# Hybrid attention and state-space kernel: three of the skips' seven products added up in PSUM, seven products for one more batch of queries, and new prices for GpSimd in the planner

## The chip, the cores and the metric

The kernel runs on one core of one Trainium2 chip. The metric is the device time of one execution in microseconds (us); "before" is the median of three runs. A profile is one further execution with the hardware profiler on. The engines are PE (TensorE, its weight loads shown as PEld), DVE (VectorE), ACT (ScalarE), POOL (GpSimd) and SP (SyncE, which issues nearly all the transfers here).

## The reference

Four layers act on `x`, a tensor of 4 sequences of 1024 tokens with 256 features, all in float32; each layer normalizes its input and adds its output to `x`.

```python
x = x + attn_a(layernorm(x), Wq, bq, Wk, bk, Wv, bv)      # causal attention, one head of 256
x = x + ffn(layernorm(x), W_r, W_k, W_v, mu_r, mu_k)      # r * (relu(k)**2 @ W_v), tokens mixed with the one before
x = x + attn_b(layernorm(x), A_log, W_B, W_C, D_skip, log_dt, W_in, b_in, W_out, b_out, ln_g, ln_b)
x = x + ffn(layernorm(x), W_r, W_k, W_v, mu_r, mu_k)      # the same weights again

# attn_b, a state-space layer (xn: the normalized input)
x_proj, z = split(xn @ W_in.T + b_in); z = silu(z)
x_mean = causal_convolution(x_proj @ W_B.T * dt.mean(), decay)   # 16 states
y = x_mean @ W_C.T + D_skip * x_proj
out = (y * z) @ W_out.T + b_out + residual
```

The change touches the queries of the attention and, in the state-space layer, `D_skip * x_proj` (called the skip) and its sum with `x_mean @ W_C.T` (called the states' share).

## The kernel before, in words

**Halves and names.** A sequence (batch `b`, 0 to 3) is worked in two halves of 512 tokens; half `j` runs from 0 to 7, `j = 2*b + h`. A tile of "columns" holds 512 tokens on the free axis and 256 features as two blocks (`c` or `e`, 0 and 1) of 128 partitions. A product of one 128x128 block of weights with 512 columns is one matmul in the code and two PE instructions in the trace.

**Eight or seven products.** A 256x256 weight applied to both halves of a batch is a product of 2x2 blocks: eight block products. `project_columns` (L774 in the trace) does it plainly, four for each half. `seven_products` (L830) does it in seven, by Winograd's scheme. Four of the seven use sums of weight blocks (made once, `weight_sums`), four use sums of data blocks `T1` to `T4` (made for each batch by `stream_sums`, L813, on GpSimd or VectorE). Each product `p1` to `p7` lands in a PSUM bank of its own, and VectorE adds them up (L838 plain, L840 with a bias): `c11 = p1 + p2`, `u2 = p1 + p6`, `u3 = u2 + p7`, `c21 = u3 + p4`, `c22 = u3 + p5`, `c12 = u2 + p5 + p3`. Before the change the queries of batches 2 and 3 (`qs2`, `qs3`), the gates `z` of batches 1 to 3 (`zs1` to `zs3`), the skips of batches 1 to 3 (`ss1` to `ss3`) and the keys of the last layer's batches 0 to 2 (`gks0` to `gks2`) are made so. Queries of batches 0 and 1 are made plainly by `queries` (tiles `pp_a0` to `pp_a3`).

**The states' share.** For batches 1 to 3, `mix_states_apart` multiplies `w_c` with the states in four small matmuls (contraction over 16 rows) into a pair of PSUM banks for each half (`py`, L1889). `grown` adds the skip, already in SBUF, to it on VectorE (L1899); `gated` multiplies by `z` on GpSimd or VectorE (L1903); `state_outputs` multiplies by `w_out` (tiles `pyo`).

**The planner.** No engine's order is written out by hand. The code logs units (a group of matmuls, in the order in which PE runs them) and operations (with what they need, and one or more ways: an engine and a price in us). `Order.finish` then plays the log through with these prices, with several sets of settings, keeps the plan that ends first by its own count, and emits every engine's instructions in that order. A way marked `DVE+port`, and every way of GpSimd, is taken to hold a port that the two engines share: the planner lets only one of them run at a time. PE's order of units is the order of the log; what stands on VectorE, ScalarE, GpSimd and in SP's queue, and when, follows from the prices. In PSUM, four single banks and two pairs are shared out among the units.

**The order of the units.** In the attention, step `i` (0 to 31) covers one tile of 128 queries: scores (`sc`), softmax, transposed weights through DRAM (`exps`, `pblocks`, `prT`), and the weighted sum (`po`). Between them stand values (`pv`), the first feed-forward layer's units (`f0` to `f7`), and the queries: plain ones by `both(queries, j)`, the seven products as a chain whose next product is logged by `go_on` when at least 0.8 us of other units lie between, and whose rest is logged at once ahead of the first scores of that batch. `attend_prepare(n)` puts the normalization of half `n`, its way through DRAM (`rows_a`, `blocks_a`) and its turn to columns (`xa`) into the log:

```python
if i == 4 * n - (12 if n % 2 and n > 2 * SEVEN_FROM else 8):
    attend_prepare(n)
```

After the attention, `more_gates(n)` takes the next `n` products of one long chain (gates and skips of batches 1 to 3), and `advance(keys, n)` the next `n` products of a chain of keys.

Of the kernel before, what the change touches and what calls it, by code (L numbers as in the profile page):

```python
# [15 lines left out]
ALU = mybir.AluOpType  # L16
# [4 lines left out]
NB = 4  # L21
# [14 lines left out]
EXP_ARG_MAX = 88.0  # L36
RPAD = P + L
APART = 0.8
SEVEN_FROM = 2
PLAIN = 1  # L40
BY_SCALAR = 6
AHEAD_FROM = 4
# [307 lines left out]
def hybrid_kernel(  # L350
# [445 lines left out]
    def stream_sums(key, src, needs):  # L796

        t = [lazy(lambda k=k: cols(f"T{k}_{key}")) for k in range(KC)]

        def b(c, h):  # L800
            return src(h)[:, c, :]

        def sums(k):
            return t[(k - 1) // 2]()[:, (k - 1) % 2, :]

        for k, plus, minus in (
            (1, lambda: b(0, 1), lambda: b(0, 0)),
            (3, lambda: b(1, 1), lambda: b(0, 1)),
            (2, lambda: b(1, 1), lambda: sums(1)),
            (4, lambda: b(1, 0), lambda: sums(2)),  # L810
        ):
            def emit(engine, k=k, plus=plus, minus=minus):
                engine.tensor_sub(sums(k), plus(), minus())  # L813

            o.op(
                f"{key}.T{k}", needs + ([f"{key}.T{k - 1}"] if k in (2, 4) else []),
                ("POOL", 1.05, partial(emit, nc.gpsimd)), ("DVE+port", dve(HALF), partial(emit, nc.vector)),
            )
        return sums

# [78 lines left out]
    class Mix:  # L899
# [4 lines left out]
        def prepare(self, j, by_hand=False):  # L904

            b, h = divmod(j, 2)
            key = f"{self.tag}{j}"
            hT = self.hT[j] = lazy(lambda: cols(f"hT_{key}", HALF + 1))
            xk = self.xk[j] = lazy(lambda: cols(f"xk_{key}"))
            xr = self.xr[j] = lazy(lambda: cols(f"xr_{key}"))  # L910
            names = [f"{key}.hT{c}" for c in range(KC)]
            self.rows[j] = normalized(
                key, b, h, self.needs(j), lambda c: hT()[:, c, 1:], names, by_hand=by_hand,
                by_scalar=self.last and j < BY_SCALAR,
            )
            if h == 0:
                first = lambda: nc.gpsimd.memset(hT()[:, :, 0:1], 0.0)
                before = [f"{key}.xn0"]
            else:
                old = self.hT[j - 1]  # L920
                first = lambda: nc.gpsimd.tensor_copy(hT()[:, :, 0:1], old()[:, :, HALF:])
                before = [f"{self.tag}{j - 1}.hT{c}" for c in range(KC)] + [f"{key}.xn0"]
            o.op(f"{key}.h", before, ("POOL", 0.2, first))
            for name, t, mu, mu1 in (("xk", xk, muk, muk1), ("xr", xr, mur, mur1)):
                for c in range(KC):
                    def scale(t=t, mu=mu, c=c):
                        nc.scalar.mul(t()[:, c, :], hT()[:, c, 1:], mu[:, c : c + 1])

                    def add(t=t, mu1=mu1, c=c):
                        nc.vector.scalar_tensor_tensor(  # L930
                            t()[:, c, :], hT()[:, c, :HALF], mu1[:, c : c + 1], t()[:, c, :],
                            ALU.mult, ALU.add,
                        )

                    o.op(
                        f"{key}.{name}m{c}", [names[c], "mu1"],
                        ("ACT", act(HALF), scale),
                        delay=0.0 if name == "xk" else 0.8,
                    )
                    o.op(  # L940
                        f"{key}.{name}{c}", [f"{key}.{name}m{c}", f"{key}.h"],
                        ("DVE+port", dve(HALF) + 0.06, add),
                    )
# [77 lines left out]
        def values(self, j, g):  # L1021
# [28 lines left out]
                f"{key}.rv{g}", [f"{key}.g{g}", f"{key}.pv{g}"], ("DVE", dve(HALF), gate),  # L1050
                frees="bank",
            )
            o.op(f"{key}.x{g}", [f"{key}.rv{g}"], ("POOL", 1.27, add))
            if last:
                o.op(None, [f"{key}.x{g}"], ("SP", 0.47, store), moves=[move(8 * P * D, 1024, True)])

# [809 lines left out]
    def skips_of_batch(b):  # L1866

        there = columns_of(2 * b) + columns_of(2 * b + 1)
        src = lambda h, xb=(xnT[2 * b], xnT[2 * b + 1]): xb[h]()
        for j in (2 * b, 2 * b + 1):  # L1870
            skips[j] = lazy(lambda j=j: cols(f"skip_{j}"))
        sb = [skips[2 * b], skips[2 * b + 1]]
        sums_of_batch(b + 1)
        yield from seven_products(
            f"ss{b}", f"zs{b}", wx_block, lambda k: x_sums[:, k - 1, :], src, sums_of_batch(b),
            lambda e, h: sb[h]()[:, e, :], lambda e: b_skip[:, e : e + 1],
            ["x_sums", "b_all"], there,
        )

    def mix_states_apart(b):  # L1880

        for h in range(2):
            py[2 * b + h] = lazy(lambda h=h: pair(f"py_{2 * b + h}"))

        def emit():
            for e in range(KC):
                for h in range(2):
                    k = 2 * e + h
                    nc.tensor.matmul(  # L1889
                        py[2 * b + h]()[:, ts(e, HALF)],  # L1890
                        lhsT=w_c[k * GRP : k * GRP + S, ts(e, P)],
                        rhs=xmT[b]()[k * GRP : k * GRP + S, ts(h, HALF)],
                        start=True,
                        stop=True,
                    )

        def grown(j, e):
            t = skips[j]()[:, e, :]
            nc.vector.tensor_add(t, py[j]()[:, ts(e, HALF)], t)  # L1899

        def gated(engine, j, e):
            t = z[j]()[:, e, :]
            engine.tensor_mul(t, t, skips[j]()[:, e, :])  # L1903

        o.unit(f"pm{b}", 1.0, ["w_c", f"xmT{b}"], emit, "pair", many=2)
        for h in range(2):
            j = 2 * b + h
            for e in range(KC):
                o.op(
                    f"g{e}.{j}", [f"pm{b}", f"ss{b}.c{e + 1}{h + 1}"],  # L1910
                    ("DVE", dve(HALF) + 0.03, partial(grown, j, e)),
                    frees="pair" if e else None,
                )
                o.op(
                    f"y{e}.{j}", [f"g{e}.{j}", f"z{e}.{j}"],
                    ("POOL", 1.05, partial(gated, nc.gpsimd, j, e)),
                    ("DVE+port", dve(HALF), partial(gated, nc.vector, j, e)),
                )

# [101 lines left out]
    for i in range(-2, NI):  # L2021
# [18 lines left out]
        if 0 < j < 2 * NB:  # L2040
# [5 lines left out]
                    attend_prepare(n)  # L2046
            if k == (1 if i < AHEAD_FROM else 0) and j < 2 * SEVEN_FROM:
                both(queries, j)
            if k == 3 and j % 2 == 1 and SEVEN_FROM <= j // 2 + 1 < NB:
                chain = queries_of_batch(j // 2 + 1)  # L2050
                behind = len(o.log)
        while valued < min(i + (3 if i < AHEAD_FROM else 4), NI - 1):
            valued += 1
# [73 lines left out]
    for b in range(NB):  # L2127
        states_in(b)
    skip(1)
    more_gates(8)  # L2130
    mix_states(0)
    more_gates(8)
    outputs(0)
    more_gates(5)
    mix_states_apart(1)
    outputs(1)
    more_gates(4)
    outputs(2)
    more_gates(4)
    mix_states_apart(2)  # L2140
    outputs(3)
    more_gates(3)
# [13 lines left out]
    keys = mix2.keys_of_batch(1)  # L2156
    both(mix2.gates, 2)
    outputs(7)
    advance(keys, 7)
    both(mix2.gates, 3)  # L2160
    both(mix2.values, 2)
    keys = mix2.keys_of_batch(2)
    both(mix2.values, 3)
# [65 lines left out]
```

## Time and profile before

| | |
|---|---|
| three runs | 464.29, 464.99, 465.58 us; median 464.99 |
| the profiled execution | 465.0 us, of which the span of its instructions is 463.1 |
| PE | busy 456.0 us, 98% of the span |
| PEld (weight loads) | busy 312.5 us, 67% |
| DVE | busy 390.2 us, 84%, 931 instructions |
| ACT | busy 220.8 us, 48%, 463 instructions |
| POOL | busy 143.1 us, 31%, 149 instructions |
| granted TensorE clock | full speed in every slice |

The span begins with the first instruction and ends with the last. A row of the groups names the line, the engine, the operation, what it writes and reads, how often it stands there, its busy time and the mean of one, and then for how long the engine had been idle before it and what ended that. VectorE starts its next instruction before the record of the last one closes: two plain adds in a row, each recorded with 0.68 us, start 0.60 us apart.

### The profile page before, as it was taken

The numbers are of one execution on the slowest core, as the hardware profiler recorded it, in microseconds if no ns is written. First come the engines' busy times: TensorE is split into PE (matmuls) and PEld (weight loads), VectorE is DVE, ScalarE is ACT, GpSimd is POOL, SyncE is SP. The second block draws the span as 40 slices with busy tenths as digits, with TensorE's granted clock in tenths as the row PEclk, the third lists the DMA queues.
The fourth block names the chain that finished last, engine by engine and source line by source line (L and its number), as shares of the span: only waits on it lengthen the run. The fifth ranks groups of instructions, "written<-read, shape, count | busy, mean of one in ns | idle before, by whom it ended". The sixth has DMA issues, their size and how long they took to land.

```text
span 463.1 us, 6634 instructions
## 1 busy us (share of the span) xinstructions
PE 456.0 (98%) x2052; PEld 312.5 (67%) x2052; DVE 390.2 (84%) x931; ACT 220.8 (48%) x463; POOL 143.1 (31%) x149
## 2 busy tenths in 40 slices
PE   8999999999999999999999999999999999999996
PEld 5766785667786667786777775474565758675875
DVE  3687769899969999889999977459889999999962
ACT  3422414454342433333556567441458777664652
POOL 3000102112013213121271354962052616826340
PEclk9999999999999999999999999999999999999999
DMA  8047876848455763427866989603022024252442
GB/s 242 21 127 203 250 190 168 222 132 258 117 135 139 221 194 93 118 62 237 224 177 182 275 268 271 260 17 88 11 92 91 1 86 144 81 147 99 129 144 84
DMA packets 84915, 69.44 MB, mean 150 GB/s; under 512 B 20160, under 2 KB 82576, under 8 KB 84880
## 3 DMA queue, kind: packets, MB, share of 16 engines
q1 hardware_dynamic: 84064, 68.76, 50.8%
q10 hardware_dynamic: 816, 0.26, 0.2%
q8 instruction: 16, 0.26, 0.2%
q14 instruction: 19, 0.16, 0.1%
HBM read 40.54 MB, written 28.45 MB: 149 GB/s over the span
## 4 chain that ended last, share of the span: by engine, by line
PE 86%; DVE 8%; issue 2%; DMA 1%; POOL 1%; ACT 1%; SPq 0%; DVEq 0%; POOLq 0%
PE po L1597 13%; PE sc L1492 13%; PE pv L1464 5%; PE p_zs L830 4%; PE p_ss L830 4%; PE p_qs L830 2%; PE p_gks L830 2%; PE py L1848 2%; PE pc L1798 2%; PE dust L1282 1%; DMA blocks_a<-rows_a 1%; PE pr_g0.pr L881 1%; PE pb L1735 1%; PE pp_a0.pq L774 1%; PE pr_g0.pv L881 1%
## 5 line engine op out<-in xcount | busy, mean ns | idle before, releaser
L1597 PE MATMUL po<-v,prT 128*128 128x256 f32 x288 | 67.7, 380 | 0.1
L1492 PE MATMUL sc<-xa,q 128*128 128x512 f32 (+3 forms) x192 | 67.0, 486 | 0.0
L1597 PEld LDWEIGHTS po<-v,prT 128*128 128x128 f32 x288 | 54.2, 189 | 11.6 <-issue 2.6
L1513 ACT ACTIVATE pr<-pr,nmx 128x128 f32<-128x128 f32 (+7 forms) x32 | 24.7, 773 | 64.6 <-DVE pr L1508 57.7
L1492 PEld LDWEIGHTS sc<-xa,q 128*128 128x128 f32 x192 | 35.1, 190 | 24.5 <-issue 19.6
L1464 PE MATMUL pv<-wv,xa 128*128 128x257 f32 x128 | 32.9, 380 | 0.0
L642 POOL TENSOR_TENSOR rs_a<-ve_a,minus_half 128x4 f32<-128x4 f32 x7 | 7.1, 1010 | 76.8 <-DVE ve_a L629 76.8
L1044 POOL TENSOR_TENSOR x<-x,r_f 128x512 f32<-128x512 f32 x16 | 20.3, 1271 | 33.0 <-DVE r_f L1038 32.5
L642 POOL TENSOR_TENSOR rs_h<-ve_h,minus_half 128x8 f32<-128x8 f32 x8 | 13.2, 1647 | 52.5 <-DVE ve_h L631 52.5
L1464 PEld LDWEIGHTS pv<-wv,xa 128*128 128x128 f32 x128 | 23.6, 191 | 7.8 <-issue 3.6
L1508 DVE TENSOR_SCALAR_CACHE_REDUCE pr<-sc,v 128x128 f32<-128x128 f32 (+7 forms) x32 | 26.2, 818 | 1.1
L1550 DVE STREAM_TRANSPOSE prT<-pblocks 128x384 f32<-128x384 f32 (+7 forms) x30 | 23.8, 793 | 2.4 <-DMA pblocks<-exps 2.3
L642 POOL TENSOR_TENSOR rs_f<-ve_f,minus_half 128x4 f32<-128x4 f32 x8 | 8.4, 1053 | 47.1 <-DVE ve_f L629 28.8
L1044 POOL TENSOR_TENSOR x<-x,r_g 128x512 f32<-128x512 f32 x14 | 18.9, 1371 | 11.0 <-DVE r_g L1038 11.0
L1641 POOL TENSOR_TENSOR x<-x,bout_r 128x512 f32<-128x512 f32 x16 | 20.0, 1279 | 4.5 <-ACT x L1634 4.5
L1606 DVE SCALAR_TENSOR_TENSOR x<-po,rsm,x 128x256 f32<-128x256 f32 x32 | 15.0, 470 | 4.3 <-PE po L1597 3.8
L1474 DVE TENSOR_TENSOR v<-pv,bv_r 128x257 f32<-128x257 f32 x32 | 13.4, 418 | 5.6 <-PE pv L1464 5.6
L930 DVE SCALAR_TENSOR_TENSOR xr_g<-hT_g,mur,xr_g 128x512 f32<-128x512 f32 x16 | 17.3, 1112 | 0.0
L663 ACT ACTIVATE xn_f<-x,mrs_f,rs_f 128x256 f32<-128x256 f32 x18 | 9.8, 592 | 15.5 <-DVE mrs_f L651 15.5
L1634 ACT ACTIVATE x<-x,mrs_h,rs 128x256 f32<-128x256 f32 x32 | 16.9, 592 | 0.0
L1903 POOL TENSOR_TENSOR z<-z,skip 128x512 f32<-128x512 f32 x9 | 13.1, 1462 | 10.9 <-DVE skip L1899 10.7
L663 ACT ACTIVATE xn_g<-x,mrs_g,rs_g 128x256 f32<-128x256 f32 x23 | 12.4, 589 | 8.3 <-DVE mrs_g L626 6.7
(458 smaller groups left out, 1089.8 us busy)
## 6 DMA issues: line engine op xcount, KB each, us to landing
hk<-r_dram SPq DMA_DIRECT2D x16, 512.0 KB, 9.2
rows_g<-xn_g SPq DMA_DIRECT2D x8, 512.0 KB, 2.9
blocks_g<-rows_g SPq DMA_DIRECT2D x32, 128.0 KB, 2.8
x<-in_L_attn_a_X_dram SPq DMA_DIRECT2D x7, 512.0 KB, 4.9
rows_f<-xn_f SPq DMA_DIRECT2D x7, 512.0 KB, 3.0
blocks_f<-rows_f SPq DMA_DIRECT2D x28, 128.0 KB, 2.7
rows_h<-xn_h SPq DMA_DIRECT2D x7, 512.0 KB, 3.7
blocks_h<-rows_h SPq DMA_DIRECT2D x28, 128.0 KB, 3.2
```

The source lines that it names most:

```text
L642: nc.gpsimd.tensor_tensor(rs()[:, :k].rearrange("p k n -> p (k n)"), ve()[:, :k].rearrange("p k n -> p (k n)"), minus_half[:, : k * NH], A ...
L663: nc.scalar.activation(place(n), split(row(n)), AF.Identity, bias=mrs()[:, k - 1, n : n + 1], scale=rs()[:, k - 1, n : n + 1],)
L830: lambda: nc.tensor.matmul(p(), lhsT=w(), rhs=data(), start=True, stop=True), "bank",
L930: nc.vector.scalar_tensor_tensor(t()[:, c, :], hT()[:, c, :HALF], mu1[:, c : c + 1], t()[:, c, :], ALU.mult, ALU.add,)
L1044: nc.gpsimd.tensor_add(xg, xg, r()[:, ts(g, 2), :])
L1464: nc.tensor.matmul(pv()[:, : D + 1], lhsT=xaj()[:, c, ts(n, P)], rhs=wv[:, c, :], start=(c == 0), stop=(c == KC - 1),)
L1492: nc.tensor.matmul(sc()[:, k * HALF : k * HALF + w], lhsT=qh()[:, c, ts(n, P)], rhs=keys[k]()[:, c, :w], start=(c == 0), stop=(c == KC - 1),)
L1508: nc.vector.tensor_scalar(dst, src, v[2 * b + h]()[:, n, D : D + 1], None, ALU.add, ALU.min, accum_out=nmx(),)
L1513: nc.scalar.activation(p()[:, :nk], p()[:, :nk], AF.Exp, bias=nmx(), scale=-1.0, accum_out=sm())
L1550: nc.vector.transpose(dst()[:, : NH * width].rearrange("p (k m a) -> p k m a", m=NH, a=GRP), blocks().rearrange("p m (k a) -> p k m a", a= ...
L1597: nc.tensor.matmul(po()[:, :D], lhsT=src()[:, ts(n, P)], rhs=v[2 * b + n // NH]()[:, n % NH, :D], start=(n == 0), stop=(n == t),)
L1641: nc.gpsimd.tensor_add(xg, xg, bout_r.unsqueeze(1).to_broadcast([P, 2, D]))
```

## The change

1. `SEVEN_FROM` goes from 2 to 1: the queries of batch 1 are made by seven products too. By the line shown above, the preparation of half 3 then enters the log at step 0 and not at step 4.
2. The chains of queries of batches 2 and 3 begin at steps 12 and 20 (`k == 0`, `j` of 4 and 6), one step later than before; that of batch 1 begins at step 4.
3. The skips' `p2`, `p4` and `p3` no longer get a bank and an add of their own. `mix_states_apart` starts each of three PSUM banks with one of them, and the states' matmul adds onto it. `skips_of_batch` keeps `p1`, `p6`, `p7`, `p5` and the adds `u2`, `u3`, `u5`, `u4`; the bias moves into `grown`.
4. The planner's prices for GpSimd change: sums `T` 1.05 to 1.45, the first column `h` 0.2 to 0.28, `x + r` 1.27 to 1.33, `gated` 1.05 to 1.4.
5. The counts of `more_gates` are fitted to the shorter chain, and the last layer's gates of half 3 are set into the chain of keys of batch 1.

```diff
-SEVEN_FROM = 2
+SEVEN_FROM = 1
...
-                ("POOL", 1.05, partial(emit, nc.gpsimd)), ("DVE+port", dve(HALF), partial(emit, nc.vector)),
+                ("POOL", 1.45, partial(emit, nc.gpsimd)), ("DVE+port", dve(HALF), partial(emit, nc.vector)),
...
-            o.op(f"{key}.h", before, ("POOL", 0.2, first))
+            o.op(f"{key}.h", before, ("POOL", 0.28, first))
...
-            o.op(f"{key}.x{g}", [f"{key}.rv{g}"], ("POOL", 1.27, add))
+            o.op(f"{key}.x{g}", [f"{key}.rv{g}"], ("POOL", 1.33, add))
...
     def skips_of_batch(b):
...
-        yield from seven_products(
-            f"ss{b}", f"zs{b}", wx_block, lambda k: x_sums[:, k - 1, :], src, sums_of_batch(b),
-            lambda e, h: sb[h]()[:, e, :], lambda e: b_skip[:, e : e + 1],
-            ["x_sums", "b_all"], there,
-        )
+        u1, u2, u3, u5 = block(0, 0), block(0, 1), block(1, 0), block(1, 1)
+        p = unit(1, lambda: wx_block(0, 0), lambda: xnT[2 * b]()[:, 0, :], there)
+        o.op(f"{key}.u1", [f"{key}.p1"], *copies(u1, p), frees="bank")
+        yield
+        p = unit(6, lambda: x_sums[:, 1, :], lambda: T(2), [f"zs{b}.T2"])
+        add("u2", 6, p, u1, u2, "u1")
+        yield
+        p = unit(7, lambda: x_sums[:, 2, :], lambda: T(3), [f"zs{b}.T3"])
+        add("u3", 7, p, u2, u3, "u2")
+        yield
+        p = unit(5, lambda: x_sums[:, 0, :], lambda: T(1), [f"zs{b}.T1"])
+        add("u5", 5, p, u3, u5, "u3", last=False)
+        add("u4", 5, p, u2, u2, "u3")
+        yield
...
     def mix_states_apart(b):
...
         def emit():
+            for h, e, w, data in (
+                (0, 0, wx_block(0, 1), xnT[2 * b]()[:, 1, :]),
+                (0, 1, wx_block(1, 1), T(4)),
+                (1, 0, x_sums[:, 3, :], xnT[2 * b + 1]()[:, 1, :]),
+            ):
+                nc.tensor.matmul(
+                    py[2 * b + h]()[:, ts(e, HALF)], lhsT=w, rhs=data, start=True, stop=False
+                )
...
-                        start=True,
+                        start=(k == 3),
...
-            nc.vector.tensor_add(t, py[j]()[:, ts(e, HALF)], t)
+            nc.vector.scalar_tensor_tensor(
+                t, py[j]()[:, ts(e, HALF)], b_skip[:, e : e + 1], t, ALU.add, ALU.add
+            )
...
-                    ("POOL", 1.05, partial(gated, nc.gpsimd, j, e)),
+                    ("POOL", 1.4, partial(gated, nc.gpsimd, j, e)),
...
-            if k == 3 and j % 2 == 1 and SEVEN_FROM <= j // 2 + 1 < NB:
-                chain = queries_of_batch(j // 2 + 1)
+            if k == 0 and j in (2, 4, 6):
+                chain = queries_of_batch(j // 2)
...
-    more_gates(8)
+    more_gates(6)
     mix_states(0)
-    more_gates(8)
+    more_gates(5)
     outputs(0)
-    more_gates(5)
+    more_gates(3)
     mix_states_apart(1)
     outputs(1)
-    more_gates(4)
+    more_gates(3)
     outputs(2)
-    more_gates(4)
+    more_gates(3)
     mix_states_apart(2)
...
-    advance(keys, 7)
-    both(mix2.gates, 3)
+    advance(keys, 4)
+    mix2.gates(3, 0)
+    advance(keys, 3)
+    mix2.gates(3, 1)
```

Built, the new kernel has one matmul fewer on PE. Against before, VectorE has 23 instructions more, GpSimd 16 fewer and ScalarE 8 fewer; SP has as many transfers as before, in another order. Of the sums `T`, GpSimd makes three in place of 15; of the `gated` products, six in place of nine.

## The prediction, made before the result was known

> **What bounds the kernel now.** I read the page first, then the waits of PE, then the timeline of PE, and last the windows.
>
> ```profile
> span 463.1 us, 6634 instructions
> PE 456.0 (98%) x2052; PEld 312.5 (67%) x2052; DVE 390.2 (84%) x931; ACT 220.8 (48%) x463; POOL 143.1 (31%) x149
> ```
>
> PE is busy for 98%, but ends of matmuls are modelled, so this alone proves nothing. The Trainium skill says so too (Perfetto Trace Analysis, Identifying the Most-Contended Engine: matmul occupancy is no measure of how near the roof is, use MFU and the share of weight loads). By that share, 67%, a third of PE would be free, and a product removed would be worth between nothing and 0.67 of itself. The timeline decides:
>
> ```profile
> 46.92 3.60 PE L774 MATMUL pp_a2.pq<-xa,wq 128*128 128x512 f32 x8
> 50.35 1.90 PE L1464 MATMUL pv<-wv,xa 128*128 128x257 f32 x8
> ```
>
> Eight instructions of 512 columns take 50.35 - 46.92 = 3.43 us, 0.429 each; so a block product (two instructions) takes 0.857 us of PE. This pitch is the same in the whole kernel. I compared every start-to-start distance of the full 128x128 matmuls with the pitch of its width: what lies above it sums to only 6.2 us. So PE does stream, and the low share of weight loads is no slack. The row counts: a product that goes is worth 0.857 us.
>
> The waits of PE:
>
> ```profile
> PE dust L1282 <- DVE idle L427: 1.2, 1, 1.2
> PE p_gks L830 <- DVE u_gks L765: 1.0, 1, 1.0
> PE pr_g2.pr L881 <- ACT r_g L1016: 0.7, 1, 0.7
> PE pp_a0.pq L774 <- DVE xa L765: 0.3, 1, 0.3
> ```
>
> Beside the start there are two: 1.0 us in the keys of batch 2 and 0.7 us in the gates of half 2 (by start-to-start 1.15 at 425.5 and 0.85 at 395.7 us). The rest of the 6.2 are bits of 0.06 to 0.2 us.
>
> ```profile
> core 0: us, PE busy (x) PEld busy (x) DVE busy (x) ACT busy (x) POOL busy (x), PEclk, DMA share, GB/s
> 140.00:260.00 120.00, 119.99 (x484) 86.44 (x483) 113.02 (x303) 51.18 (x96) 34.06 (x36) 1.00 0.60 170
> 330.00:380.00 50.00, 49.97 (x183) 31.49 (x182) 45.61 (x77) 35.11 (x111) 18.72 (x22) 1.00 0.17 54
> 380.00:430.00 50.00, 48.33 (x197) 35.62 (x196) 47.56 (x78) 31.84 (x64) 27.57 (x24) 1.00 0.41 126
> ```
>
> VectorE is the second bound: idle for 7.0 us of 120 in the second half of the attention, 4.4 of 50 and 2.4 of 50 in the late stages. And that is where PE loses time: the 1.15 us wait is made by VectorE waiting for GpSimd.
>
> ```profile
> 421.67 1.61 POOL L813 TENSOR_TENSOR T_gks<-xk_g,T_gks 128x512 f32<-128x512 f32 x1 [2.12 <-issue]
> 423.28 3.81 POOL L1044 TENSOR_TENSOR x<-x,r_g 128x512 f32<-128x512 f32 x3
> 422.06 1.24 DVE L651 SCALAR_TENSOR_TENSOR mrs_g<-rs_g,mv_g 128x4 f32<-128x4 f32 x1
> 423.23 1.51 DVE L657 TENSOR_SCALAR xn_g<-x,mv_g,rs_g 128x256 f32<-128x256 f32 x1
> 424.66 0.68 DVE L765 COPY u_gks<-p_gks 128x512 f32<-128x512 f32 x1
> 425.48 1.10 PE L830 MATMUL p_gks<-T_gks,w_fk 128*128 128x512 f32 x2 [0.98 <-DVE u_gks L765]
> ```
>
> A 4-column `mrs` takes 1.24 us (0.15 elsewhere) and `xn` 1.51 (0.40 elsewhere): both end as a GpSimd instruction ends. The copy that frees PE's bank stands behind them.
>
> **The change part by part.** PE's own work. Queries of batch 1: eight products leave (the rows `pp_a2`, `pp_a3`, 2 x 3.43 us), seven enter: -0.86 us. Skips: seven products become four in banks and three in the pairs, the states' four matmuls stay: 0.
>
> VectorE, in starts (adds 0.60, with a bias 0.66, `xn` 0.33):
> - Skips, for each of three batches: seven adds become four, and four `grown` gain a bias. 4 x 0.66 + 7 x 0.60 becomes 4 x 0.60 + 4 x 0.66: -1.8 each, -5.4. One of the three first copies moves here from ScalarE: +0.6.
> - Queries of batch 1: seven adds (4.4) and three of the four sums (1.8) in place of four ScalarE copies; one copy of half 1 leaves for ScalarE: +5.5.
> - Other sums `T`, from GpSimd: seven of the keys, five of the gates, one of the queries: 13 x 0.60 = +7.9.
> - Three `gated` +1.8, six `xn` from ScalarE +2.0.
>
> Sum +12.4 us. GpSimd loses 16 instructions. Their shortest record, alone, is 1.27 us:
>
> ```profile
> L813 POOL TENSOR_TENSOR T_gks<-xk_g x2: 1268/1268/1269, 367.3 to 399.7; 128x512 f32<-128x512 f32 x2
> L813 POOL TENSOR_TENSOR T_zs<-xnT,T_zs x3: 1597/1627/1724, 289.5 to 314.5; 128x512 f32<-128x512 f32 x3
> L813 DVE TENSOR_TENSOR T_zs<-xnT,T_zs x3: 692/1640/1753, 288.7 to 315.0; 128x512 f32<-128x512 f32 x3
> ```
>
> What that gives back: of the 64 mixes of L930, 52 run free at 738 ns and 12 beside a long GpSimd instruction at 1240; so 6.0 us lost there, and in the same way 4.1 at L813, 5.5 at L651, 4.4 at L657, 1.8 at L626: 21.8 us, or 0.22 for each of some 100 long GpSimd instructions. The skill's page SBUF — State Buffer (Who interferes with whom) calls it an exclusive lock: a VectorE instruction with two SBUF inputs and a GpSimd one that reads SBUF block each other for a whole instruction; Perfetto Trace Analysis (Optimizing Scalar/DVE Operations) adds that moving work between these two might not help. That speaks against the 16 moves. By the rule's worst, a full 1.27 us block each, they would free 20 us of VectorE; by the row 16 x 0.22 = 3.5, plus most of the 4.1 at L813, where both engines made sums at once: 3.5 to 7.6. I take 5, the row's side. So VectorE gains about 7.5 us and stands near 398 us, 86%.
>
> Where it falls. (a) Half 3's preparation comes four steps earlier, its rows write, four block reads and two turns too, past loads and the exponentials in SP's queue, into a stretch with a DMA share of 0.81 to 0.87 (before, it was turned at 63.7 us). Adding up issue and landing times of before (2.8 us for a read), its blocks land near 42.6 us and are turned near 45.3: 2.7 us of cover. If they came later than that, VectorE would stand in front of the mask of `sc` and PE a few us after. (b) The chain of batch 1 ends in five products back to back ahead of its first scores, which need `c21`. From the rows of the timeline: `p4` ends near 56.3, `c21` is added near 57.6, PE asks near 58.0. No wait, margin 0.4 us. Between it and PE stand two turns of `prT` (1.0 and 1.1 us). (c) The chains of batches 2 and 3 the same; the later start also takes away 0.22 us at 92.9, where PE stood for `blocks_a`. Three bursts in place of spread products cost 0 to 0.5 us each; I take 0.2 each, as the margins come out positive. (d) From 140 to 260 us VectorE gains 4.5 us, most of it `xn` and the chain of batch 3, and has 7.0 idle: no bound, but thin; I take +0.3. (e) From the first `pyo` to `g5` VectorE gains 9.2 us before relief, on a PE stretch that is 4.2 us longer (products of the skips come later). Idle of before 7, lengthening 4.2, relief 3 to 5: it fits with about 6 left. Added wait: the states' unit now also waits for `T4` and the columns, all made before, and takes its pairs 2.6 us earlier; `grown` of the batch before is over by then. (f) The two waits: the copy `u_gks` of batch 2 is now on ScalarE, which has 18 of 50 us free, and the adds of `pyo` come sooner behind `pr_g2`: -1.7 of the 2.0. But all four sums of batch 2 and three of batch 1 of the keys are VectorE's: `p7` of batch 1 comes within 0.3 us of its sum; +0.4.
>
> Sum: -0.86 - 0.22 - 1.7 + 0.6 + 0.3 + 0.4 = -1.5; small waits of 0.06 to 0.2 us around the skips' chain (0.9 us between 340 and 380), of which fewer adds take a third, make it -1.8. Against the profiled 465.0 (span 463.1 and 1.9 around) that gives 463.2; the median of the runs shown, 464.99, is the same number.
>
> **The rivals.** Only the product counts: the two waits go, but others of their size come with the bursts: -0.86 to -1.3, 463.7 to 464.2. For it: every stall that I take away was made by VectorE, which gets more work. Against it: the largest blocks, GpSimd's, become fewer. VectorE becomes the bound between 165 and 260 us and from 340 us on: its gain there is 4.5 + 9.2 us. It decides from the point where relief is under 1 us and idle time can't be filled (before never more than 97% in a stretch of 30 us): then PE waits for 2.5 us in the late stage and 1 in the attention, and with -0.86 the time is 467.0 or more. For it: 47.56 of 50. Against it: the longer PE stretch, and that GpSimd falls from 27.6 to about 20 there. The change doesn't do what it says, since the planner fills what it thinks free: the orders show the moves made, so only the prices can be off. A GpSimd sum beside VectorE took 1.6, not 1.45; that is inside the second case.
>
> **How the numbers follow.** This kernel's measurement tells 0.3% (1.4 us) from no change; so faster is below 463.6. The forecast, 463.2: 0.5, of which a part lies as low as 461 (all waits of the late stage gone). Only the product: 0.27, half of it on either side of the line. VectorE as the bound: 0.23, 465.5 to 468. This gives faster 0.55, same 0.24, slower 0.21. The likeliest case alone holds 461.5 to 464.0; the range goes to 466.6 for the others.
>
> **What would show it.** Right: PE has two instructions fewer; no wait of PE for `u_gks` or `r_g`; VectorE 395 to 400 us, POOL near 120; mean of L930 `xr_g` below 1112 ns. Wrong: new rows of PE waiting for DVE at `p_qs`, `sc` or `po` between 45 and 60 us (half 3 late), or at `p_gks` near 402 (sums late), or VectorE over 98% between 165 and 260 us with PE gaps there.

## The result, and the profile after

The changed kernel took 473.14 us (median of four runs, 471.26 to 475.12) where the kernel before took 465.28 (median of four): ratio 1.0169, 95% interval 1.0144 to 1.0195. It is 8 us slower; the forecast was 463.2, with a range up to 466.6. Here is its profiled execution (472.17 us), first from the page:

```profile
span 470.4 us, 6642 instructions
PE 455.6 (97%) x2050; PEld 312.6 (66%) x2050; DVE 395.5 (84%) x954; ACT 216.5 (46%) x455; POOL 122.5 (26%) x133
```

The sums by engine are what was forecast: PE two instructions fewer, VectorE 395.5, GpSimd 122.5. Read alone, this page would say that nothing happened. The waits of PE (us in total, times, longest) say what did:

```profile
PE pt_f7.hT L756 <- ACT xn_f L663: 2.4, 1, 2.4
PE pp_g6.pk L774 <- DVE xk_g L930: 2.4, 1, 2.4
PE po L1597 <- DVE q L838: 1.5, 1, 1.5
...
PE pt_f7.hT L756 <- DVE xn_f L657: 0.8, 1, 0.8
PE po L1597 <- ACT w_xt L764: 0.7, 1, 0.7
```

The two waits of before (`p_gks` for `u_gks`, `pr_g2.pr` for `r_g`) are gone. Five others stand there, none of which was in the kernel before. The windows of after, in the columns of the windows shown ahead:

```profile
140.00:260.00 120.00, 118.82 (x479) 85.39 (x478) 110.92 (x303) 49.37 (x94) 32.86 (x34) 1.00 0.61 166
380.00:430.00 50.00, 50.00 (x202) 36.92 (x202) 47.56 (x84) 30.79 (x60) 19.27 (x17) 1.00 0.34 108
430.00:470.00 40.00, 34.24 (x135) 25.29 (x133) 24.63 (x48) 15.61 (x26) 9.11 (x8) 0.96 0.35 112
```

From 380 to 430 us PE now loses nothing (48.33 of 50 before), as forecast. From 140 to 260 us VectorE is busy for less time than before (110.92 against 113.02), and yet PE loses there: VectorE isn't full, it is late.

**The account.** I took PE's excess again (start-to-start distance above the pitch of the width), this time with the distance behind the 64 small `pd` products, which the prediction's sum had left out; before then has 6.5 us and not 6.2. In all 20 profiles of this case the span less this excess lies between 455.0 and 458.3 us. So, to within 3 us, the excess tells how long a kernel takes, and its place tells where it lost time. In us, by stretch:

| kernel | 0-100 | 100-165 | 165-255 | 255-340 | 340-end | sum |
|---|---|---|---|---|---|---|
| before | 0.8 | 0.5 | 0.5 | 1.2 | 3.5 | 6.5 |
| after | 0.2 | 2.6 | 2.2 | 5.5 | 4.8 | 15.3 |

The excess grew by 8.8 us; the span grew by 7.3, since a product is gone (0.86 us) and since PE's transposes of the second weight (`pt_wk_n`) started 0.76 us earlier in this execution (5.71 against 6.47 us). A kernel below that keeps the order of before through the attention (new skips and new prices, order held) started them at 5.82: that is scatter between executions.

**255 to 340 us.** The last half's transposes `pt_f7.hT` waited for 3.6 us (to 264.0 us, and again to 265.1); another 0.7 us went at the transposes `pt_h7.T` at 293 us. From the timeline of after:

```profile
253.80 2.54 PE L1597 MATMUL po<-v,prT 128*128 128x256 f32 x11
255.07 1.40 DVE L930 SCALAR_TENSOR_TENSOR xk_f<-hT_f,muk,xk_f 128x512 f32<-128x512 f32 x2
256.39 1.41 DVE L930 SCALAR_TENSOR_TENSOR xr_f<-hT_f,mur,xr_f 128x512 f32<-128x512 f32 x2
259.50 1.05 DVE L657 TENSOR_SCALAR xn_h<-x,mv_h,rs_h 128x256 f32<-128x256 f32 x3
260.54 0.48 DVE L1606 SCALAR_TENSOR_TENSOR x<-po,rsm,x 128x256 f32<-128x256 f32 x1
263.18 2.16 DVE L657 TENSOR_SCALAR xn_f<-x,mv_f,rs_f 128x256 f32<-128x256 f32 x3
263.28 1.27 POOL L1044 TENSOR_TENSOR x<-x,r_f 128x512 f32<-128x512 f32 x1
263.95 0.33 PE L756 MATMUL pt_f7.hT<-ident,xn_f 128*128 128x128 f32 x1 [2.44 <-ACT xn_f L663]
```

And of before:

```profile
245.62 1.41 DVE L930 SCALAR_TENSOR_TENSOR xk_f<-hT_f,muk,xk_f 128x512 f32<-128x512 f32 x2 [0.16 <-ACT xk_f L927]
248.12 1.37 DVE L930 SCALAR_TENSOR_TENSOR xr_f<-hT_f,mur,xr_f 128x512 f32<-128x512 f32 x2
255.22 0.48 DVE L1606 SCALAR_TENSOR_TENSOR x<-po,rsm,x 128x256 f32<-128x256 f32 x1 [0.43 <-PE po L1597]
257.79 2.13 DVE L657 TENSOR_SCALAR xn_f<-x,mv_f,rs_f 128x256 f32<-128x256 f32 x3
259.76 0.14 PEld L756 LDWEIGHTS pt_f7.hT<-ident,xn_f 128*128 128x128 f32 x1 [0.24 <-DVE xn_f L657]
```

In before, VectorE stood ready and waited 0.43 us for the last `po`. In after, `po` is done near 256.3 us and its addition `x` starts at 260.54: VectorE was working through the last of the mixes of half 6 (to 257.8), the statistics of three tiles and three `xn_h` (to 260.5). In before it did these mixes at 245.6 to 249.5 us. Its place in the queue is fixed when the kernel is built: the addition stood behind all of these, and so it started 4.2 us after its `po` was done. So 4 us of work that PE was not waiting for stood in front of an instruction that PE waited for. How it fell behind, from the timeline a little earlier:

```profile
239.51 1.11 DVE L1550 STREAM_TRANSPOSE prT<-pblocks 128x896 f32<-128x896 f32 x1 [1.94 <-DMA pblocks<-exps]
240.54 1.25 DVE L1038 SCALAR_TENSOR_TENSOR r_f<-r_f,pr_f4.pv 128x512 f32<-128x512 f32 x2
241.71 0.14 DVE L651 SCALAR_TENSOR_TENSOR mrs_f<-rs_f,mv_f 128x4 f32<-128x4 f32 x1
241.78 3.11 DVE L657 TENSOR_SCALAR xn_f<-x,mv_f,rs_f 128x256 f32<-128x256 f32 x3
241.87 2.55 POOL L1044 TENSOR_TENSOR x<-x,r_f 128x512 f32<-128x512 f32 x2 [1.52 <-DVE mrs_f L651]
```

`mrs_f` was issued behind a turn that waited 1.94 us for its DMA (in before it ran at 232.75, ahead of that turn), and three `xn_f` then took 3.11 us, two of them beside GpSimd's additions, where three `xn_h` above took 1.05. Counted over the attention: the 20th addition `x` of VectorE is 3.2 us earlier than in before, the 32nd 5.3 us later.

**100 to 255 us.** The chain of batch 2, at its end:

```profile
111.62 0.71 DVE L840 SCALAR_TENSOR_TENSOR q<-p_qs,bm,q 128x512 f32<-128x512 f32 x1
112.25 1.40 DVE L930 SCALAR_TENSOR_TENSOR xk_f<-hT_f,muk,xk_f 128x512 f32<-128x512 f32 x2
113.56 0.69 DVE L838 TENSOR_TENSOR q<-p_qs,q 128x512 f32<-128x512 f32 x1
114.30 2.00 PE L1597 MATMUL po<-v,prT 128*128 128x256 f32 x8 [1.52 <-DVE q L838]
```

Not the scores wait for the chain, but the next `po`: it needs the bank that the chain's last addition frees, and that addition stands behind two mixes. The chain of batch 3 does the same at 180.9 us (0.54 before `pt_wx`); the 0.83 us before the `po` that follows at 182.3 is put down to ScalarE's copy of what `pt_wx` made (the row `w_xt` above), so it comes one step behind the chain.

**The last gates.** VectorE's mixes for `pp_g6` came late, and one of them took 1.75 us beside GpSimd:

```profile
441.42 2.40 DVE L930 SCALAR_TENSOR_TENSOR xk_g<-hT_g,muk,xk_g 128x512 f32<-128x512 f32 x2
441.64 1.64 POOL L1044 TENSOR_TENSOR x<-x,r_g 128x512 f32<-128x512 f32 x1 [0.37 <-DVE r_g L1038]
443.97 5.37 PE L774 MATMUL pp_g6.pk<-xk_g,w_fk 128*128 128x512 f32 x8 [2.37 <-DVE xk_g L930]
```

```profile
444.00:448.00 4.00, 4.00 (x6) 1.68 (x7) 3.38 (x6) 0.48 (x1) 2.11 (x2) 0.57 0.64 190
```

The wait is 2.5 us, and then the granted clock is 0.57 on average over the four microseconds that follow (second fence, the window 444 to 448): products of 512 columns start 0.85 us apart, not 0.43, which loses another 1.8 us. Together 4.3 us.

### The profile page after: what moved, and what is told of

Its sections match the earlier page's. It is cut to its first block, busy times and chain, and to the rows that moved or that the text cites. A ratio compares the mean times of both kernels' runs of the same rounds, so it can differ in the third digit from the quotient of the medians.

```text
span 470.4 us, 6642 instructions
## 1 busy us (share of the span) xinstructions
PE 455.6 (97%) x2050; PEld 312.6 (66%) x2050; DVE 395.5 (84%) x954; ACT 216.5 (46%) x455; POOL 122.5 (26%) x133
## 4 chain that ended last, share of the span: by engine, by line
PE 65%; DVE 16%; DMA 10%; issue 3%; SPq 3%; ACT 2%; DVEq 0%; ACTq 0%
PE sc L1492 7%; PE po L1597 7%; PE p_zs L830 4%; PE pv L1464 4%; PE p_gks L830 3%; PE p_ss L1882 2%; DVE xn_f L657 2%; PE p_qs L830 2%; PE py L1920 2%; DMA blocks_h<-rows_h 2%; PE py L1848 2%; PE pc L1798 2%; SPq L725 1%; DMA exps<-pr 1%; DMA rows_f<-xn_f 1%
## 5 line engine op out<-in xcount | busy, mean ns | idle before, releaser
L927 ACT ACTIVATE xk_f<-hT_f,muk 128x512 f32<-128x512 f32 x16 | 10.9, 718 | 18.2 <-DVE hT_f L731 17.1
L642 POOL TENSOR_TENSOR rs_g<-ve_g,minus_half 128x4 f32<-128x4 f32 x8 | 9.0, 1123 | 30.8 <-DVE ve_g L621 20.1
L930 DVE SCALAR_TENSOR_TENSOR xk_g<-hT_g,muk,xk_g 128x512 f32<-128x512 f32 x16 | 13.3, 866 | 3.1 <-ACT xk_g L927 3.0
L663 ACT ACTIVATE xn_h<-x,mrs_h,rs_h 128x256 f32<-128x256 f32 x18 | 9.8, 590 | 12.5 <-DVE mrs_h L651 9.2
```

Source lines behind the costliest of these rows:

```text
L642: nc.gpsimd.tensor_tensor(rs()[:, :k].rearrange("p k n -> p (k n)"), ve()[:, :k].rearrange("p k n -> p (k n)"), minus_half[:, : k * NH], A ...
```

## Experiments: undoing one part at a time

The kernels ran in groups of two or four, each group on one chip and beside the kernel before; the groups ran on four chips, on which the kernel before took 464.6 to 465.2 us.

**Old prices** (after, with the four numbers of before):

```
-("POOL", 1.45, ...T...)    -("POOL", 0.28, first)   -("POOL", 1.33, add)   -("POOL", 1.4, ...gated...)
+("POOL", 1.05, ...T...)    +("POOL", 0.2, first)    +("POOL", 1.27, add)   +("POOL", 1.05, ...gated...)
```

> The changed kernel with GpSimd's four prices as they were (1.05, 0.2, 1.27, 1.05). Theory 'prices': the higher prices put sums and normalisations on VectorE, whose queue runs 4 to 9 us late at 250 us and at 440 us, so PE stood 3.6 us before the last transposed half and 4.3 us before the last gates; with the old prices at least half of these 8 us come back: 464 to 469 us. Theory 'places' (the later, denser query chains and the skips' new form cost it, wherever the sums are computed): 471 to 474 us.

Measured: 469.21 us, ratio 1.0089 (1.0071 to 1.0106). Half of the loss comes back, 0.2 us short of the first theory's range.

**Old chain start** (after, with the line of before):

```
-            if k == 0 and j in (2, 4, 6):
-                chain = queries_of_batch(j // 2)
+            if k == 3 and j % 2 == 1 and SEVEN_FROM <= j // 2 + 1 < NB:
+                chain = queries_of_batch(j // 2 + 1)
```

> The changed kernel with each query chain started one step earlier again (after the last value product of the step before). Theory 'chain': the sums and adds of the late chain of batch 3 fall together with the turns of the probabilities, VectorE is then 5 us behind until 262 us; started earlier, the 3.6 us wait at 264 us and the 3.4 us lost between 100 and 182 us go: 466 to 468 us. Theory 'prices' or 'skips': 471 to 474 us.

Measured: 476.61 us, 1.0253 (1.0231 to 1.0275): slower still, and outside both ranges. But the excess from 165 to 255 us fell to 0.5 us and that from 100 to 165 to 1.0. So the waits of the bursts go with the later start, as expected. The wait at 264 us is gone as well, as the first theory had it, but the stretch 255 to 340 kept 5.8 us: they are now lost 30 us later, at the transposes `pt_h7.T` (290 to 294 us).

```profile
PE p_qs L830 <- DVE xa L731: 3.0, 2, 2.5
PE pt_h7.T L756 <- ACT xn_h L663: 1.8, 1, 1.8
...
PE pt_h7.T L756 <- DVE xn_h L657: 1.8, 1, 1.8
```

And 3.2 us came new ahead of 100 us (batch 1's chain, now started before its blocks were turned: the first row).

**Two batches by seven products** (after, with batch 1 by eight):

```
-SEVEN_FROM = 1
+SEVEN_FROM = 2
...
-            if k == 0 and j in (2, 4, 6):
+            if k == 0 and j in (4, 6):
```

> The changed kernel with batch 1's queries by eight products again (seven products from batch 2 on). One product more: +0.86 us of PE. Theory 'seven costs more than it saves' (5.5 us of VectorE work between 30 and 100 us): 470 us or less. If only the product counts: 473 to 475 us.

Measured: 473.67 us, 1.0195 (1.0173 to 1.0216), within the range of "only the product counts". Batch 1 by seven is not what costs 8 us. (But its losses stand at other places: 2.5 us at 257 us, and 0.8 in place of 3.6 at `pt_f7.hT`.)

**The new skips alone** (before, with the change from the skips on: `skips_of_batch`, `mix_states_apart`, the counts of gates, the keys split by a gate):

```
-    more_gates(8)
+    more_gates(6)
...
-    advance(keys, 7)
-    both(mix2.gates, 3)
+    advance(keys, 4)
+    mix2.gates(3, 0)
+    advance(keys, 3)
+    mix2.gates(3, 1)
```

> The kernel before with the change of the skips and what stands behind the attention alone (products closed in the states' pairs, fewer gate products between the batches, keys split by a gate); prices, queries and chains as before. By the prediction's step (f) the two waits of 0.85 and 1.15 us go: 463 to 464.5 us. Theory 'the late stage of the change is bad in itself' (its last gates wait 4.3 us): 466 to 469 us.

Measured: 476.16 us, 1.0262 (1.0229 to 1.0295). Both theories missed: and its excess from 255 to 340 us is 9.9 us. Of these, 3.8 are lost at 262.8 us and 3.1 at 292 to 296, where the source is that of before: the first product of a skip comes later (313 us in before). An edit of the last third had made the middle slow. None of the three parts undone brings the time back, and one part alone costs more than all together. That made me drop the theory that a part of the change is to blame. What all of them have in common is the planner: it sets VectorE's, ScalarE's and GpSimd's order for the whole kernel, tries 20 settings of (share, margin, wait) and takes the one that it reckons the shortest. An edit anywhere can change the setting, and so every queue. The kernel before takes (0.1, 2.5, 0.22), after and the two batches (0.1, 2.5, 0.15), the old prices and the old chain (0.1, 1.5, 0.15), the skips alone (0.1, 1.5, 0.22).

## Experiments: the order, with nothing edited

Each of these kernels is given one setting in place of the list, for instance:

```
-    PLANS = [
-        (share, margin, wait)
...
+    PLANS = [(0.1, 1.5, 0.22)]
```

**The kernel before at (0.1, 1.5, 0.22)**:

> The kernel before, its source unchanged but for the planner's list of settings: it may only use (share 0.1, margin 1.5, wait 0.22), the setting that the kernel with the new skips alone was given, in place of (0.1, 2.5, 0.22), which the kernel before is given. Theory 'order': any re-ordering of VectorE's queue costs what was lost, since the order before was an unusually good one, and the edits are innocent: 469 to 476 us. Theory 'edits': the setting alone is worth under 2 us, 463 to 467 us.

Measured: 477.03 us, 1.0258 (1.0225 to 1.0292). The page, and PE's waits:

```profile
span 478.1 us, 6625 instructions
PE 462.9 (97%) x2052; PEld 315.0 (66%) x2052; DVE 400.6 (84%) x944; ACT 215.4 (45%) x451; POOL 142.5 (30%) x148
```

```profile
PE p_gks L826 <- DVE T_gks L809: 2.8, 2, 1.6
PE pt_h7.T L752 <- DVE xn_h L653: 2.6, 3, 1.4
PE pt_f7.hT L752 <- DVE xn_f L653: 1.6, 1, 1.6
PE pp_g6.pk L770 <- DVE xk_g L926: 1.5, 1, 1.5
```

The same source, the same 2052 products, another order, and the time is 12 us longer. Two of the waits are those of after: `pt_f7.hT` for `xn_f` and `pp_g6.pk` for `xk_g`. So these two are places where this kernel loses time when the order is not a good one, changed or not. A third is seen more often: `pt_h7.T`, near 290 us, lost 1.6 to 4.0 us in 11 of the 20 profiles (this one among them), nothing in before and 0.7 in after. (PE's 462.9 busy us are again a lower clock behind waits, see the end.)

**The changed kernel at the setting of before, (0.1, 2.5, 0.22)**:

> The changed kernel, held to the setting (0.1, 2.5, 0.22) that the kernel before is given; by itself it takes (0.1, 2.5, 0.15). Theory 'order': the good setting brings most of the 8 us back, 464 to 468 us. Theory 'prices': VectorE has the same 13 sums more, 470 us or more.

Measured: 485.25 us, 1.0444 (1.0425 to 1.0462), the slowest of all, as only the second theory's range allows. So there is no good setting to be carried over; what is good is one order, of one source. My theory had that wrong.

**The new skips alone at (0.1, 2.5, 0.22)**:

> The kernel with the new skips alone (as in the earlier run), held to the setting (0.1, 2.5, 0.22) of the kernel before; free, it took (0.1, 1.5, 0.22), and lost 5.9 us at 260 to 268 us and 3.7 us at 290 to 297 us, in stretches whose source is unchanged. Theory 'order': these two losses go, 463 to 467 us. Theory 'edits': 473 us or more.

Measured: 470.94 us, 1.0131 (1.0113 to 1.0149), in between. The loss from 255 to 340 us fell from 9.9 to 2.8 us.

**Old prices at (0.1, 2.5, 0.22)**:

> The changed kernel with the old prices of GpSimd (469.2 us with the setting that it took, (0.1, 1.5, 0.15)), held to (0.1, 2.5, 0.22). Theory 'order': under 467 us. Theory 'edits' (chains and skips cost the rest): 468 to 470 us.

Measured: 475.88 us, 1.0245 (1.0225 to 1.0265), 6.7 us above the same source at the setting that it takes by itself, and above both ranges. Again only the order differs.

**Pairs at equal setting.** Of four settings both kernels were run; three of these runs are these:

```
-    PLANS = [ ... ]
+    PLANS = [(0.1, 2.5, 0.15)]      # before
+    PLANS = [(0.1, 1.5, 0.15)]      # before, after
+    PLANS = [(0.1, 1.5, 0.22)]      # after
```

> The kernel before, unedited, all of it planned with the setting (0.1, 2.5, 0.15), the one that the changed kernel took. Theory 'order' (before's 465 us is one good order among many worse): 468 to 480 us, near the changed kernel's 473. Theory 'edits': 466 us or less, so that the change costs its 8 us at equal setting.

> The kernel before, unedited, planned with (0.1, 1.5, 0.15). Theory 'order': 468 to 480 us. Theory 'edits': 466 us or less.

> The changed kernel planned with (0.1, 1.5, 0.15), beside the kernel before at the same setting. Theory 'order': the pair differs by chance, with either sign, both within 468 to 480 us. Theory 'edits': 5 us or more above its partner.

> The changed kernel planned with (0.1, 1.5, 0.22), where the kernel before took 477.0 us. Theory 'order': 468 to 482 us, above or below. Theory 'edits': 482 us or more.

| setting | before, us | after, us | difference |
|---|---|---|---|
| (0.1, 2.5, 0.22) | 464.8 | 485.25 | +20.4 |
| (0.1, 2.5, 0.15) | 467.27 | 473.14 | +5.9 |
| (0.1, 1.5, 0.15) | 469.28 | 472.51 | +3.2 |
| (0.1, 1.5, 0.22) | 477.03 | 475.70 | -1.3 |

Before scatters over 12 us by its order and its own is the best of the four; after scatters over 13. In the last pair the two can't be told apart (the six runs of before lie between 474.35 and 479.91). At (0.1, 2.5, 0.15) the kernel before, at 467.27, lies between the two theories. But three of four differences are positive (mean of the four +7), so "order alone" isn't the whole either.

The planner can't tell these orders apart. Its own count, worked out by the kernel's source, is 454.8, 457.0, 457.1 and 454.9 us for the four orders of before, from the top of the table down: the one that it puts second, 0.1 us behind the first, is the slowest by far. For after as it stands it counts 454.6, 0.2 us less than for before.

The prices can be paired in the same way. With the old ones after took 469.21 at (0.1, 1.5, 0.15), where with the new ones it took 472.51, and 475.88 at (0.1, 2.5, 0.22) against 485.25. So in both pairs the new prices cost 3 to 9 us, each time with another order under them.

Where it may not be chance, the stretches show: from 100 to 255 us the four before have an excess of 0.8 to 1.0 us, the four after 4.4, 4.8, 5.8 and 8.6. That part, 3.5 us and more against 0.86 saved, came with the change in all four orders. Of the parts undone above, only the old chain start takes it away (1.5 us, where after at the same setting, (0.1, 1.5, 0.15), has 4.4); with the old prices the two stretches still have some 4 us, and with batch 1 by eight some 5. From 340 us on they overlap (before 3.5 to 9.4, after 4.8 to 12.1). From 255 to 340 us before has 1.2, 1.4, 1.9 and 8.9, after 5.4 to 6.8: likely a cost of the change, but one order of before is worse.

## Experiments: the order held, one part edited

The planner's decisions for the kernel before were written down (which operation on which engine, in which order), and these kernels replay them up to the first product of the skips' batch 1; what stands behind is planned as usual. That product starts at 313 us in the trace of before (the expectations below say 340), so the last 27 us of the stretch 255 to 340 are planned anew:

```
+HELD = """ ... """.split()          # before's steps up to that product: engine and number
...
     def _step(self):
+        if self.held < len(HELD):
+            way, n = HELD[self.held][0], int(HELD[self.held][1:])
...
+            self.held += 1
+        else:
             self.at, k = self._first()
```

**New skips, order held:**

> The new skips alone (old prices, queries and chains as before), and VectorE, ScalarE, GpSimd and SyncE keep the order of the kernel before up to the first product of the skips' batch 1 at about 340 us; only what stands behind is planned anew. Theory 'order': without the re-ordering of the first 340 us nothing is lost there (PE's excess before 340 us under 3 us), and the time is that of the late stage, 462.5 to 467 us. Theory 'edits': the new skips cost by themselves, 470 us or more.

Measured: 467.21 us, 1.0045 (1.0030 to 1.0061). The excess ahead of 340 us is 3.7 us (11.7 when all was planned anew, 3.0 in before): 8 us of loss in the same source are gone with the order alone. Both figures lie a little above what 'order' expected (467 and 3 us).

**New skips and new prices, order held** (all that the change does to the late stage):

> As the run before (order of the first 340 us held), with the new prices of GpSimd as well: what the change does to the late stage, alone. Theory 'prices': the sums of keys and gates go to VectorE, which is late at the last gates by 2 to 4 us, 466 to 470 us. Theory 'order': the same as with the old prices, within 1.5 us.

Measured: 464.55 us over 22 runs, ratio 0.9988 (0.9979 to 0.9997). The page and PE's waits:

```profile
span 461.8 us, 6620 instructions
PE 454.0 (98%) x2052; PEld 312.0 (68%) x2052; DVE 384.7 (83%) x943; ACT 216.4 (47%) x454; POOL 122.2 (26%) x134
```

```profile
PE dust L1442 <- DVE idle L587: 1.2, 1, 1.2
PE pr_g3.pv L1041 <- DVE ka_g L1151: 1.0, 1, 1.0
PE pt_h7.T L916 <- ACT xn_h L823: 0.5, 1, 0.5
```

This is the only version that is faster than the kernel before, by 0.6 us; its late excess is 2.2 us against 3.5. VectorE has 12 instructions more than before and is busy for 5.5 us less; GpSimd has 134 instructions against 149, and what VectorE's instructions lose beside it fell by some 10 us. Both theories missed: with the prices the late stage came out 2.7 us shorter than with the old ones, and the order under it differs too.

**The same, at another setting for the late stage:**

```
+    PLANS = [(0.1, 1.5, 0.22)]
```

> The new skips with the new prices and the order of the first 340 us held (464.55 us with the setting that it took, (0.1, 1.5, 0.15)), its late stage planned with (0.1, 1.5, 0.22). Theory 'order': the late stage scatters by its setting as that of the kernel before does, 464 to 469 us. If the new late stage is better whatever the order: 463 to 465 us.

Measured: 470.66 us, 1.0120 (1.0100 to 1.0140), beyond the range of either: the excess behind 340 us is 8.4 us. So the 0.6 us above are also one order's, not a property of the new skips. The kernel before, its late stage planned at the same setting, is 2.5 us faster (next).

**The kernel before, late stage at (0.1, 1.5, 0.22), order held:**

> The kernel before, nothing edited, its order held up to 340 us, and only the late stage planned with the setting (0.1, 1.5, 0.22). All over, that setting gave 477.0 us, of which PE's excess behind 340 us was 9.2 us and before 340 us 10.7 us. Theory 'order': it falls to between 466 and 472 us (the late stage's part alone). Theory 'luck of the chip, not the order': 464 to 466 us.

Measured: 468.18 us, 1.0053 (1.0032 to 1.0074). Of the 12 us that this setting cost all over, 3.0 are left (against the 465.19 measured beside it) when only the late stage follows it, as 'order' expected.

## Experiments: one edit alone, all planned anew

**Prices alone** (before, with the four new prices):

> The kernel before with the four new prices alone, all planned anew (it takes the setting (0.2, 2.5, 0.22)). Theory 'prices': at least as slow as the whole change, 472 to 480 us, with sums and normalisations moved from GpSimd and ScalarE to VectorE. If the prices are better because they are nearer to what was measured: 463 to 467 us.

Measured: 471.83 us, 1.0143 (1.0127 to 1.0159). That is 0.2 us below the range of 'prices' and far from the other. At 100 to 165 us it loses nothing (0.3), from 165 to 255 1.6 us, from 255 to 340 3.5 us (1.8 of them at `pt_h7.T`), from 340 us on 7.8. The kernel before was not run at its setting, so how much of this is the prices' and how much the order's is open.

**Chains alone** (before, with batches 2 and 3 started later):

```
-            if k == 3 and j % 2 == 1 and SEVEN_FROM <= j // 2 + 1 < NB:
-                chain = queries_of_batch(j // 2 + 1)
+            if k == 0 and j in (4, 6):
+                chain = queries_of_batch(j // 2)
```

> The kernel before with the start of the query chains of batches 2 and 3 one step later, and nothing else (all planned anew; it takes (0.1, 1.5, 0.15), at which the unedited kernel took 469.3 us). Theory 'bursts cost': PE loses 0.8 to 1.8 us between 100 and 140 us and 1 to 2.5 us between 180 and 220 us, where unedited kernels lose 0.2 and 0.1 to 0.4 us; 470 to 475 us. Theory 'bursts are free' (the prediction's 0.2 us each): under 0.5 us in each stretch, 467 to 470 us.

Measured: 471.08 us, 1.0128 (1.0109 to 1.0146). Two of its waits of PE:

```profile
PE pr_g5.pr L881 <- DVE u_gks L838: 2.1, 1, 2.1
...
PE po L1597 <- ACT w_xt L764: 0.7, 1, 0.7
```

It lies 1.8 us above the kernel before at the same setting (469.28), which is inside the time that 'bursts cost' gave. But the bursts alone cost 0.3 us near 114 and 0.84 near 181 us, together 1.1, less than that theory had. They are cheap by themselves. With the rest of the change they are not: from 100 to 255 us it has an excess of 1.5 us without the later start (the old chain start above) and 4.8 with it (4.4 at equal setting). The rest of its loss lies behind 340 us (excess 8.5 against 3.5), in source that it shares with before: the re-ordering again.

## Why the prediction was wrong, point by point

- **The sums were right, and did not matter.** PE's product: -0.86, read off between `pp_a1` and `pp_f0` (their distance is 0.86 us shorter). VectorE 395.5 (forecast 395 to 400). GpSimd 122.5 (near 120). Relief from GpSimd: the five lines that lost 21.8 us lose 14.5 (L930 3.0, L813 3.0, L657 7.0, L651 1.5, L626 0), and two other lines lose 2.4: 4.9, where 5 was taken and, by the prediction's estimate, the exclusive lock of the Trainium skill (SBUF — State Buffer, Who interferes with whom) would have had up to 20. Mean of `xr_g` 744 ns, below 1112. Half 3's blocks (a) made no wait. The late waits (f): -1.7 forecast; from 380 to 430 us the excess fell from 2.5 to 0.2.
- **The step that failed is that the rest of the kernel would stay as it was.** The prediction read the orders for what was added, removed and moved to another engine, and said of them that "the orders show the moves made, so only the prices can be off". It did not ask of the instructions that both kernels have, whether they kept their places. They had not: the mixes of half 6 stood ahead of the addition of the last attention tile but one in before and behind it in after, and ran 9 us later; the addition `x` of the last tile ran 5.3 us later, and PE waited 3.6 us for what hangs on it. The queue's order is fixed when the kernel is built, so the new places were there to be read; what could not be read from them was the price, and no case of the prediction held room for it. It came to +8.8 us of PE's excess where the prediction had some -1. The unedited kernel moves over 12 us by its order alone (464.8 to 477.0), more than twice the width of the range that was forecast, and before's own order was the best of the four that were run: part of the 8 us may be that a lucky order was given up.
- **(d), from 140 to 260 us, +0.3.** The term measured +1.7 from 165 to 255 us, and 3.6 more at 264 us that come from there. Two things were mis-sized. Six `xn` at 0.33 made +2.0; up to the last attention addition VectorE had 18 `xn_f` in place of 11, and they kept it busy for some 6 us more: five of the 18 took 1.35 to 1.51 us beside GpSimd's additions, where one of the 11 did, and the others 0.37 to 0.41. And the idle 7.0 us were taken as room. An engine whose order is fixed can't use idle time that lies in front of a wait: VectorE ended up with more idle time than before, not less (6.8 us in gaps above 0.15 us from 140 to 266 us, against 4.9), and was late all the same.
- **(b) and (c), three bursts at 0.2.** The scores were checked for being late, and they weren't. Batch 1's burst cost nothing, and the sign named for it (waits at `p_qs`, `sc` or `po` between 45 and 60 us) did not come. The wait is of the next user of a bank for the chain's additions: of the chain's own next product (0.62 us near 108), of `po` (1.52 near 114) and of `pt_wx` (0.54 near 181), with 0.83 us more at the `po` behind it: 3.5 us for batches 2 and 3 where 0.4 was taken.
- **The rivals.** "VectorE becomes the bound between 165 and 260 us and from 340 us on" named the places. Its mechanism (too much work) did not hold, since VectorE's share is 84% as before; late in its queue is not full. And its price, 2.5 and 1 us, was a third of what stood there and at the bursts ahead of it: 4.3 at the last gates, 3.6 at 264 us and 3.5 at the bursts.
- **What stays open.** No kernel could keep before's order through the attention with the attention edited, since the recorded steps no longer fit. So how much of the loss at 255 to 340 us is the edit's and how much the draw's is not settled: four draws against four overlap there, and the loss moves between `pt_f7.hT` and `pt_h7.T` from one order to the next. Why the later chain start costs 1 us alone and some 3 with the rest of the change is not settled either, nor whether the new prices cost by themselves: all planned anew they did in both pairs, with the order held up to 313 us they did not.

## What to carry to other kernels

When a planner in the kernel orders several in-order queues, an edit is worth its own cost plus a new draw of the whole order, and the second can be the larger: measure the draw first, by running the unedited kernel at another setting. Compare edits with the order held, by replaying the recorded order up to the place of the edit, and write down a good order once it is found rather than let it be drawn again. A busy share says nothing of lateness: look for the instruction that PE waits for, and at what stands ahead of it in its queue.

## What the runs showed of the hardware that I had not expected

A wait of PE can cost nearly twice its length. After the wait of 2.5 us at 444.0 us the clock record of the trace has half the clock for 3.41 us, and that cost another 1.8 us. But it does not follow each time: behind the 2.6 and 1.0 us at 264 us of the same profile the clock stayed at 1.00, and so it did behind a wait of 2.4 us at 447.3 us in the kernel with two batches by seven. In the kernel before at (0.1, 1.5, 0.22) three places at half pace (from 263, 294 and 437 us) cost some 4 us. In the 20 profiles such stretches lie ahead of the last matmul 14 times, and each is 3.41 or 6.83 us long. Both waits of 3.8 us (the skips alone, to 262.8 us, and after at (0.1, 2.5, 0.22), to 443.1 us) were followed by one. So were shorter ones: in the kernel with the old prices PE's longest idle time ahead of the stretch at 291 us was 0.9 us, but three waits in a row left it busy for only some 40% of the 3.4 us before.

The Trainium skill (TensorE: Matmul & The Clock Gate, Part 1: The HAM clock gate) has TensorE at half its clock after at least one idle window of some 3.4 us, in windows that run freely. The length of the stretches agrees with such a window, and that the same wait is punished once and not another time agrees with its running freely. That PE has to be idle for a whole window does not hold here: 12 of the 14 stretches followed idle times of 0.9 to 2.4 us.
